# A graph layer over a dense adjacency on one core: one shift of the quick weights on GpSimd, two pairs of copies ordered, the order of all work drawn anew

## The chip, the cores and the metric

The kernel runs on one core of one Trainium2 chip. The time is device microseconds of one execution; three runs of the kernel before took 192.53, 192.82 and 192.81 us, median 192.81. The profile is of a fourth execution, of 192.34 us, whose span from the first to the last instruction is 190.6 us.

## What is computed

The reference, cut to what matters (4096 nodes, 64 features, an adjacency `adj` of 4096 x 4096 float32 zeros and ones):

```python
h = maximum(layernorm(x), 0)
support = h @ weight
mask = (adj != 0)
rank = cumsum(mask, axis=1)
deg = rank[:, -1:]
k = minimum(deg, 100)
pos = rank - (deg - k)
w = mask * where(pos > 0, 0.5 ** (k - pos), 0)
out = x + (w @ support + bias)
```

`k - pos` is the number of neighbours that stand further right in the same row. So each neighbour is weighted by a power of two whose exponent is a count of ones behind it, and only the last 100 neighbours of a row count.

## The kernel before

**Tiles and units.** The adjacency is 64 MB and is read once, as 64 tiles of 128 rows by 2048 columns (1 MB each). Four tiles that cover 512 rows and one half of the columns are a unit; there are 16 units, `u` = 0 to 15, two for each of eight groups `g` of 512 rows. A group's right half comes first, because counts run from the right. Unit 15 is the left half of the last group; its tiles are 60 to 63.

**The way of a tile n.** `load` (L120, SP's queue, eight buffers) brings it. `convert` packs four columns as bytes into one 32-bit word (L341 on DVE; for the tiles in `signed` L339 on ACT, with one more bit operation in `settle`, L361). `transpose` turns 128x128 words through TensorE into PSUM (L352). `settle` copies them to `mt` (L363, DVE).

**The way of a unit u.** `totals` sums the bytes over short stretches (L369, PE). Two bytes of these sums are turned to float16: the first by `split` (L379, ACT), the second by `divide` (L382, DVE), both out of the same PSUM tile and into the two halves of one tile `sums`. In a left half `carry` (L388, GpSimd) puts the counts of the right half into row 0. `suffix` (L396, PE) adds what lies behind each stretch, and `clamp` (L400, DVE) limits that to 100. `place` (L407 and L412, PE) adds the counts within a stretch and leaves in each of four PSUM tiles `v` two bytes per element that are the exponents; a unit has two calls of it, for k = 0 to 3 and for k = 4 to 7. There are five buffers `v`, taken in turn.

**Weights and sums.** For each k `weigh` (L420, ACT) makes the weights by one exponential of 128x1024 values. `aggregate` (L457, PE) multiplies them with the features `hr` into the accumulator of the group, two matmuls for each k. In the last unit k = 5, 6, 7 are weighed and multiplied in two halves of 256 rows each (third argument 0 and 1). Three weights, `QUICK` = (14,4), (15,0), (15,4), are made on DVE instead: `encode` (L426) multiplies the count by minus 2^23 and limits it, `cut` (L431) adds 100 times 2^23 so that the integer is the bit pattern of the power of two, `take` (L435) copies that to the type of the matmul; `gather` is their `aggregate`, with features that `lower` (L443, GpSimd) has scaled.

**The end of a group.** `drain` adds the bias and copies the accumulator to SBUF (L473 on ACT), `turn_back` transposes it (L480), `finish` adds it to x (L487 and L488, DVE). For the last group, g = 7, all three come in two halves: the drain's first half on ACT, its second on DVE (L471), and each half has its own store (L490). `store` (L495) writes the other rows from SP's queue, behind the loads.

**What sets the order.** A planner at the end of the function lists every step as `task(step, arguments, engine, rank, hold, lag, needs, pool)`. `hold` and `lag` are the nanoseconds for which a step is taken to hold its engine and until its result is there; `needs` are the steps before it. `shift` and `own` are tables that move the rank of a kind of step and of a single step. A loop builds the order: it takes the engine that can start soonest and, among the steps that it could start within that engine's window (`wait`), the one of lowest rank.

```python
free = [1200, 3400, 4000, 5500, 800]
wait = 250, 60, 250, 60, 0
...
_, at, kind = min((rank, at, kind) for at, rank, e, kind in heads if e == engine and at <= soon + wait[engine])
```

The times of the planner live only in it. What reaches the chip is the order of instructions on each engine, which is kept, and semaphore waits for the data and the buffers.

Of the kernel before, what the change touches and what calls it, by code (L numbers as in the profile page):

```python
# [13 lines left out]
I32 = mybir.dt.int32  # L14
# [3 lines left out]
ALU = mybir.AluOpType  # L18
# [13 lines left out]
def kernel(  # L32
# [34 lines left out]
    nc = tc.nc  # L67
# [260 lines left out]
    low, codes, masks, words, wts, accs, tots, pts, sums8, behind, vs, signed = {}, {}, {}, {}, {}, {}, {}, {}, {}, {}, {}, (2, 8)  # L328
# [100 lines left out]
    def cut(u, k):  # L429

        nc.vector.tensor_scalar(codes[u, k][:, 1].bitcast(I32), codes[u, k][:, 0].bitcast(I32), 100 * 2.0 ** 23, None, op0=ALU.add)  # L431
# [60 lines left out]
    def store(r):  # L492
# [8 lines left out]
    shift = {"aggregate": 45, "carry": -26.5, "center": 25, "clamp": -23.5, "constants": 43.5, "convert": 36, "cut": 18.5,  # L501
             "divide": 0.5, "drain": -44.5, "encode": -1, "finish": -29.5, "first": -47.5, "halved": 5, "lower": 10.5,
             "order_of": 19.5, "power": -19.5, "relu": 39.5, "root": 26.5, "scale": 31, "second": 23.5, "settle": -26,
             "split": -38.5, "spread": 12, "square": 48.5, "store": 8, "suffix": 25, "support": 70, "take": -12, "totals": -32,
             "transpose": -15.5, "turn": 20, "turn_back": 62, "turned": 29, "weigh": 24}
    own = {
           "aggregate": {(0, 0): 6, (0, 3): -2, (0, 4): -16, (0, 6): -11, (1, 0): 7, (1, 1): -18, (1, 5): -5, (1, 7): -9, (11, 4): 10, (11, 5): 14, (11, 6): 6, (11, 7): -1, (12, 0): -20, (12, 3): 4, (12, 4): -2, (12, 5): -4, (12, 6): -10, (13, 1): -10, (13, 2): 6, (13, 3): 8, (13, 4): 1, (13, 5): -12, (13, 6): -4, (13, 7): -12, (14, 0): 2, (14, 1): 1, (14, 2): -16, (14, 3): -11, (14, 4): 15, (14, 5): -8, (14, 6): 18, (14, 7): -36, (15, 2): -4, (15, 3): -2, (15, 4): 1, (15, 5): 1, (15, 5, 0): -1, (15, 5, 1): -6, (15, 6): 8, (15, 6, 0): 7, (15, 6, 1): -3, (15, 7): -2, (2, 1): 4},
           "carry": {(1,): -2, (13,): 6, (15,): 3, (3,): 29}, "center": {(0,): 1, (1,): 2, (2,): 1, (3,): 3},
           "clamp": {(0,): -13, (1,): -8, (13,): 7, (15,): -14, (2,): -8, (3,): -2}, "constants": {(0,): -17, (1,): 15},
           "convert": {(1,): 20, (12,): -12, (13,): 4, (14,): -4, (16,): 19, (17,): 8, (18,): -16, (19,): -4, (2,): -9, (20,): -1, (4,): 5, (5,): 9, (57,): -16, (58,): -5, (59,): 8, (6,): -1, (60,): -5, (61,): -1, (7,): 1, (8,): 16, (9,): 8},  # L510
           "count": {(2,): 1}, "counted": {(2,): -18, (4,): 8}, "cut": {(14, 4): 15},
           "divide": {(0,): 24, (1,): 2, (14,): 8, (15,): -14, (2,): 15, (3,): -4},
           "drain": {(0,): 8, (5,): -22, (6,): 6, (7, 0): 7, (7, 1): 4}, "encode": {(14, 4): -9},
           "finish": {(5,): 7, (6,): -33, (7, 0): 4, (7, 1): -1}, "first": {(0, 0): -1, (1, 0): 1, (1, 1): 8},
           "halved": {(0,): -3, (1,): -5, (13,): 4, (14,): -9, (2,): 4}, "lower": {(15, 0): -3}, "order_of": {(2,): 4, (4,): 3},
           "place": {(0, 0): -8, (0, 1): -8, (1, 0): -13, (12, 1): 1, (13, 0): 8, (13, 1): -2, (14, 0): -9, (14, 1): 5, (15, 0): -26, (15, 1): 2, (2, 0): -4, (2, 1): 16},
           "power": {(): -23}, "relu": {(0,): -4, (1,): -3, (2,): 8}, "root": {(): -7}, "scale": {(3,): -6},
           "second": {(0, 0): -6, (0, 1): -1, (1, 1): 22},
           "settle": {(1,): -4, (10,): 2, (11,): 1, (12,): -9, (13,): 19, (15,): 2, (17,): -2, (18,): -19, (19,): -6, (2,): -11, (3,): 6, (4,): -11, (5,): -4, (56,): 5, (57,): 22, (58,): -2, (59,): 5, (6,): 1, (61,): -4, (63,): -4, (9,): 1},
           "split": {(0,): 5, (1,): -9, (13,): 3, (14,): 9, (15,): 3, (2,): -1, (3,): -12},  # L520
           "spread": {(0,): 10, (1,): 14, (2,): -9, (3,): -1}, "square": {(1,): 10, (2,): -5, (3,): -12},
           "store": {(0,): -13, (1,): -3}, "suffix": {(1,): 3, (13,): -36, (14,): -6, (15,): -1}, "support": {(0,): -3, (2,): 15},
           "take": {(15, 0): -4, (15, 4): -2},
           "totals": {(0,): -1, (1,): -4, (13,): 3, (14,): -4, (15,): 10, (2,): -2, (3,): 7, (4,): -15},
           "transpose": {(0, 0, 2): 4, (0, 2, 4): -9, (1, 0, 2): -8, (10, 0, 2): -16, (11, 0, 2): 7, (11, 2, 4): 14, (12, 0, 2): -2, (12, 2, 4): -18, (13, 0, 2): -1, (13, 2, 4): 4, (14, 0, 2): -16, (15, 0, 2): -1, (15, 2, 4): 5, (16, 2, 4): -14, (17, 0, 2): -12, (18, 0, 2): 29, (18, 2, 4): 29, (19, 0, 2): 16, (19, 2, 4): -4, (2, 0, 2): -2, (2, 2, 4): 1, (3, 2, 4): -15, (4, 0, 2): 3, (4, 2, 4): 21, (5, 0, 2): -4, (5, 2, 4): -4, (56, 0, 2): 1, (56, 2, 4): -1, (57, 0, 2): -27, (58, 0, 2): 1, (58, 2, 4): 8, (59, 0, 2): 5, (6, 0, 2): 25, (6, 2, 4): 37, (60, 2, 4): -7, (61, 0, 2): 10, (61, 2, 4): 6, (63, 0, 2): -8, (7, 0, 2): -2, (8, 0, 2): -1, (8, 2, 4): -16, (9, 2, 4): -1},
           "turn": {(0, 0): -12, (0, 12): 10, (0, 4): 2, (0, 8): 3, (1, 0): -25, (1, 4): -16},
           "turn_back": {(5,): 4, (6,): -22, (7, 0): 8}, "turned": {(0, 0): 2, (0, 12): 6, (1, 12): -6, (1, 4): 12, (1, 8): 14},
           "weigh": {(0, 2): 8, (0, 3): 3, (0, 4): 3, (0, 5): 4, (0, 7): -16, (1, 0): 22, (1, 3): -3, (1, 4): 1, (1, 7): 2, (12, 3): 8, (12, 4): -8, (12, 5): -6, (12, 6): -22, (12, 7): 6, (13, 0): 2, (13, 1): -12, (13, 2): 23, (13, 5): 10, (13, 6): -8, (13, 7): 5, (14, 3): -3, (14, 5): -4, (14, 7): -8, (15, 2): -4, (15, 3): -11, (15, 5, 0): 3, (15, 5, 1): -19, (15, 6): 7, (15, 6, 0): -3, (15, 6, 1): -4, (15, 7): -5, (15, 7, 0): 4, (15, 7, 1): 3, (2, 0): 2, (2, 1): 4, (2, 3): -7, (2, 4): 8, (2, 6): 2, (2, 7): -1, (3, 0): -4, (3, 1): 1}}
# [50 lines left out]
    for u, (g, c0, cb) in enumerate(UNITS):  # L579
# [3 lines left out]
        task(divide, (u,), DVE, at - 2.5, 600, 720, [("totals", u)])  # L583
# [5 lines left out]
        for k in range(2 * cb):  # L589
            due = at + k  # L590
            if k % 4 == 0:
                task(place, (u, k // 4), PE, due, 800, 920, [("clamp", u), ("constants", 1)], ("v", *(("encode" if (u, k + j) in QUICK else "weigh", u, k + j, *((1,) if u == U - 1 and k + j in PARTED else ())) for j in range(4))))
            if u == U - 1 and k in PARTED:
                continue
            weighs = "weigh"
            piece_of = block(u, k) // (HB // 2)
            if (u, k) in QUICK:
                weighs = "take"
                task(encode, (u, k), DVE, due - 8, 1150, 1270, [("place", u, k // 4), ("convert", NT - 2)])
                task(cut, (u, k), DVE, due - 8, 650, 770, [("encode", u, k)])  # L600
                task(take, (u, k), DVE, due - 8, 650, 770, [("cut", u, k)], ("w", ("gather", u, k)))
                task(lower, (u, k), POOL, due - 8, 1200, 1300, [("second", piece_of // 2, piece_of % 2), ("convert", NT - 3)])
            else:
                task(weigh, (u, k), ACT, due + 2.5, 1000, 1130, [("place", u, k // 4)], ("w", ("aggregate", u, k)))
            task(gather if (u, k) in QUICK else aggregate, (u, k), PE, due + 14, 480, 720, [(weighs, u, k), ("lower", u, k) if (u, k) in QUICK else None, ("second", piece_of // 2, piece_of % 2)] +
                 ([("drain", g - 1)] if g and head and k == 0 else []))
        for part in range(2 if u == U - 1 else 0):
            for k in PARTED:
                due = at + k + part
                task(weigh, (u, k, part), ACT, due + 2.5, 520, 650, [("place", u, k // 4)], None if part else ("w", ("aggregate", u, k, 1)))  # L610
                task(aggregate, (u, k, part), PE, due + 14, 260, 500, [("weigh", u, k, part)])
        if c0 == 0:
# [5 lines left out]
            else:  # L618
                for part in range(2):
                    task(drain, (g, part), DVE if part else ACT, at, 300, 350, [("aggregate", u, PARTED[-1], part), *(("gather", *uk) for uk in QUICK)])  # L620
# [9 lines left out]
    wait = 250, 60, 250, 60, 0  # L630
    landed, taken, order = 0, {p: [] for p in places}, []
    while kinds:
# [16 lines left out]
        if f in (load, fetch):  # L649
            lag = max(landed - at, 2450) + (1280 if f is fetch else 620 * UNITS[UT[args[0]][0]][2])  # L650
            lag += 1400 if key == ("load", 6) else 0
# [49 lines left out]
```

## Time and profile before

| | us | |
|---|---|---|
| median of three runs | 192.81 | 192.53 to 192.82 |
| span of the profiled execution | 190.6 | granted TensorE clock 0.98 |
| PE busy | 172.4 | 90% of the span, 1504 matmuls |
| DVE busy | 165.6 | 87%, 225 instructions |
| ACT busy | 158.1 | 83%, 175 instructions |
| GpSimd busy | 19.7 | 10%, 60 instructions |
| `weigh`, L420, 128x1024 | 126.7 | 122 x 1120 ns |
| `convert` on DVE, L341 | 86.2 | 62 x 1393 ns |
| `convert` on ACT, L339 | 5.0 | 2 x 2511 ns |
| `settle`, L363 | 42.2 | 62 x 681 ns |
| `split`, L379 / `divide`, L382 | 9.6 / 11.0 | 16 x 598 / 16 x 685 ns |
| `encode` / `cut` / `take` | 3.7 / 2.1 / 2.1 | 3 x 1224 / 693 / 691 ns |

Read it as an average over a stretch with transfers and a tail without them. Busy shares of 83 to 90% on three engines say that no engine is idle for long, not which of them sets the end. The slices of the span, the landing times of the loads and the waits in the last 23 us tell that. A matmul's recorded end is modelled, and recorded spans of GpSimd are rough. An ACT instruction's recorded span overlaps the next one's by about 0.1 us, so a row of them is counted by the spacing of starts.

### The profile page before, as it was taken

What the parts mean: (1) busy time and instruction counts of PE and PEld (TensorE: products, weight loads), DVE (VectorE), ACT (ScalarE), POOL (GpSimd) and SP (SyncE); (2) the same over time, 40 slices, a digit from 0 to 9 for tenths busy, and PEclk for the clock granted to TensorE, in tenths of its full rate; (3) what the DMA queues carried; (4) which work ended last, traced back from release to release, by engine and by line L of the source; (5) the groups of instructions that cost most, each with busy time, mean ns of one, the idle gap of its engine ahead of it and who ended that gap; (6) DMA issues with size and microseconds to landing.
All of it is one profiled execution on the core that took longest, in us unless ns stands there. A gap on an engine that the chain in (4) does not pass through costs nothing.

```text
span 190.6 us, 3811 instructions
## 1 busy us (share of the span) xinstructions
PE 172.4 (90%) x1504; PEld 106.5 (56%) x1504; DVE 165.6 (87%) x225; ACT 158.1 (83%) x175; POOL 19.7 (10%) x60
## 2 busy tenths in 40 slices
PE   7799999787988999999999989999999898989981
PEld 5676959254644565556664645655565454644460
DVE  4853886999999998999999988999999999988753
ACT  2289219999897899889987999989989799998880
POOL 7000062100000000100010002000100058001000
PEclk9999859999999999999999999999999999999999
DMA  6999999999999999999999999999999999902000
GB/s 211 418 419 423 418 419 428 409 418 423 423 413 423 425 413 425 423 414 425 421 411 426 421 414 425 423 419 416 423 416 418 423 418 418 381 27 83 0 3 28
DMA packets 10338, 69.49 MB, mean 365 GB/s; under 512 B 1360, under 2 KB 1616, under 8 KB 2128
## 3 DMA queue, kind: packets, MB, share of 16 engines
q1 hardware_dynamic: 10016, 69.15, 87.8%
q8 instruction: 12, 0.20, 0.4%
q10 hardware_dynamic: 304, 0.10, 0.2%
q14 instruction: 6, 0.05, 0.1%
HBM read 68.19 MB, written 1.05 MB: 363 GB/s over the span
## 4 chain that ended last, share of the span: by engine, by line
PE 45%; ACT 14%; DVE 13%; issue 12%; DMA 8%; POOL 7%; POOLq 0%; ACTq 0%; DVEq 0%
PE acc L457 16%; ACT wk L420 11%; PE pt L352 9%; DMA a_sb<-in_adj_dram 8%; DVE m L341 5%; PE v L412 4%; PE v L407 4%; POOL low L443 3%; PE tot L369 2%; PE ps L396 2%; PE pd L281 2%; DVE mt L363 2%; PE pc L265 2%; PE px L256 2%; DVE xs L307 1%
## 5 line engine op out<-in xcount | busy, mean ns | idle before, releaser
L420 ACT ACTIVATE wk<-v,floor 128x1024 fp32r<-128x1024 uint8 (+1 forms) x128 | 130.2, 1101 | 13.1 <-PE v L412 12.8
L341 DVE TENSOR_SCALAR m<-a_sb 128x2048 uint8<-128x2048 f32 x62 | 86.2, 1393 | 2.6 <-DMA a_sb<-in_adj_dram 2.6
L457 PE MATMUL acc<-wk,hr 128*128 128x512 f32 (+1 forms) x256 | 78.5, 421 | 1.4 <-ACT acc_sb L473 0.9
L457 PEld LDWEIGHTS acc<-wk,hr 128*128 128x128 f32 x256 | 43.2, 189 | 14.6 <-issue 3.3
L352 PE MATMUL pt<-ident,m 128*128 128x128 f32 x256 | 42.2, 286 | 6.9 <-DVE m L341 2.8
L363 DVE COPY mt<-pt 128x512 uint32<-128x512 uint32 x62 | 42.2, 681 | 5.8 <-PE pt L352 5.7
L352 PEld LDWEIGHTS pt<-ident,m 128*128 128x128 f32 x256 | 28.5, 143 | 25.2 <-issue 8.2
L388 POOL COPY sums<-behind 1x512 f16<-1x512 f16 x8 | 6.1, 766 | 133.5 <-ACT sums L379 133.5
L407 PE MATMUL v<-behind,where 32*128 32x512 f16 x128 | 14.8, 390 | 1.2 <-DVE behind L400 0.6
L412 PE MATMUL v<-mt,tri 32*32 32x512 f16 x512 | 14.4, 401 | 0.0
L379 ACT ACTIVATE sums<-tot 128x512 f16<-128x512 uint8 x16 | 9.6, 598 | 5.1 <-DVE sums L382 2.7
L400 DVE TENSOR_SCALAR behind<-ps,excess 128x512 f16<-128x512 f32 x16 | 11.9, 743 | 0.8 <-PE ps L396 0.7
L382 DVE CAST sums<-tot 128x512 f16<-128x512 uint8 x16 | 11.0, 685 | 1.6 <-ACT sums L379 0.9
L396 PE MATMUL ps<-sums,later 128*128 128x512 f16 x32 | 10.1, 398 | 0.8 <-POOL sums L388 0.7
L369 PE MATMUL tot<-mt,band 128*32 128x512 f16 x128 | 10.2, 393 | 0.1
L412 PEld LDWEIGHTS <-tri 32*32 32x32 f16 x512 | 4.4, 88 | 10.0 <-issue 10.0
L407 PEld LDWEIGHTS <-where 32*128 32x128 f16 x128 | 3.7, 91 | 10.6 <-issue 10.6
L248 PE MATMUL none<-junk 128*128 128x256 bf16 x49 | 8.0, 334 | 1.1 <-DVE junk L133 1.1
L260 ACT ACTIVATE mt<-px 64x512 f32<-64x512 f32 x8 | 4.2, 585 | 4.8 <-PE px L256 4.8
L248 PEld LDWEIGHTS <-junk 128*128 128x128 bf16 x49 | 5.8, 120 | 3.2 <-DVE junk L133 1.1
L473 ACT ACTIVATE acc_sb<-acc,bias_sb 128x512 f32<-128x512 f32 (+1 forms) x8 | 5.3, 664 | 1.5 <-PE acc L457 1.4
L480 PE MATMUL po<-ident,acc_sb 128*128 128x128 f32 x30 | 4.8, 280 | 1.4 <-ACT acc_sb L473 1.4
(88 smaller groups left out, 98.6 us busy)
## 6 DMA issues: line engine op xcount, KB each, us to landing
a_sb<-in_adj_dram SPq DMA_DIRECT2D x64, 1024.0 KB, 15.6
xr<-in_x_dram SPq DMA_DIRECT2D x2, 512.0 KB, 6.3
out_dram<-xr SPq DMA_DIRECT2D x1, 512.0 KB, 18.6
out_dram<-xr SPq DMA_DIRECT2D x1, 384.0 KB, 2.3
out_dram<-xr ACTq DMA_DIRECT2D x1, 64.0 KB, 1.6
out_dram<-xr SPq DMA_DIRECT2D x1, 64.0 KB, 1.6
w<-in_L_gnn_weight_dram ACTq DMA_DIRECT2D x2, 16.0 KB, 6.0
bias_sb<-in_L_gnn_bias_dram SPq DMA_DIRECT2D x1, 0.2 KB, 15.7
```

What stands on the lines that cost most here:

```text
L248: nc.tensor.matmul(none[:, :2 * P], junk[:, :P], junk, start=True, stop=True)
L341: nc.vector.tensor_scalar(m_v, a_v, 0.0, 64.0, op0=ALU.not_equal, op1=ALU.add)
L352: nc.tensor.transpose(pts[n][:, c, :], m32[:, c * P:(c + 1) * P], ident)
L363: nc.vector.tensor_copy(mw, pt)
L369: nc.tensor.matmul(tot[SUB * c:SUB * (c + 1), :], band[:, SUB - 12 - 4 * a:2 * SUB - 12 - 4 * a], masks[u][:, c, :, a], start=(a == 0), st ...
L382: nc.vector.tensor_copy(*bytes_of(u, 1))
L396: nc.tensor.matmul(px, later[cb][:r, f, :], sums[:r, f, :], start=(f == 0), stop=(f == 1))
L400: nc.vector.tensor_scalar(behind[u], pts.pop((u, "s")), excess[UNITS[u][2]], float(MAX_NEIGH), op0=ALU.subtract, op1=ALU.min)
L407: nc.tensor.matmul(v, where[q, a, :], behind[u][q, :], start=True, stop=False, skip_group_check=True)
L412: nc.tensor.matmul(vs[u, 4 * a + j][SUB * c:SUB * (c + 1), :], tri[q, q], m, start=False, stop=True, skip_group_check=True)
L420: nc.scalar.activation(wts[u, k][:, :, r], v.bitcast(U8).rearrange("p (i f) -> p f i", f=4)[:, :2, r], AF.Exp, scale=-LN2, bias=floor)
L457: nc.tensor.matmul(accs[g][:, r], parts.rearrange("p s d -> p (s d)"), wk[:, s, r], start=(k == s == 0 and c0 + cb * E * P == N), stop=(c0 ...
```

## The change

It has these parts.

- `signed` has the tiles 0, 1, 6 and 13 instead of 2 and 8: four converts run on ACT, sixty on DVE.
- `cut` is issued on GpSimd instead of DVE, for all three quick weights.
- `divide` needs `split` in the planner, instead of `totals`; `drain` of the last group's second half needs the first half.
- The holds and lags of `divide`, `encode`, `take`, the halved `weigh` and the halved `drain` are larger, ACT's window in the planner is 150 instead of 250, and the landing of load 54 is taken to be 1400 later, as that of load 6 already was.
- Nearly all entries of `shift` and `own` are other numbers.

```diff
-    low, codes, ..., signed = {}, {}, ..., (2, 8)
+    low, codes, ..., signed = {}, {}, ..., (0, 1, 6, 13)
...
-        nc.vector.tensor_scalar(codes[u, k][:, 1].bitcast(I32), codes[u, k][:, 0].bitcast(I32), 100 * 2.0 ** 23, None, op0=ALU.add)
+        nc.gpsimd.tensor_scalar(codes[u, k][:, 1].bitcast(I32), codes[u, k][:, 0].bitcast(I32), 100 * 2.0 ** 23, None, op0=ALU.add)
...
-    shift = {"aggregate": 45, "carry": -26.5, "center": 25, "clamp": -23.5, ...
+    shift = {"aggregate": 60, "carry": -21, "center": 30, "clamp": -28, ...
...
-        task(divide, (u,), DVE, at - 2.5, 600, 720, [("totals", u)])
+        task(divide, (u,), DVE, at - 2.5, 610, 730, [("split", u)])
...
-                task(encode, (u, k), DVE, due - 8, 1150, 1270, [...])
-                task(cut, (u, k), DVE, due - 8, 650, 770, [("encode", u, k)])
-                task(take, (u, k), DVE, due - 8, 650, 770, [("cut", u, k)], ("w", ("gather", u, k)))
+                task(encode, (u, k), DVE, due - 8, 1160, 1300, [...])
+                task(cut, (u, k), POOL, due - 8, 1800, 1900, [("encode", u, k)])
+                task(take, (u, k), DVE, due - 8, 690, 820, [("cut", u, k)], ("w", ("gather", u, k)))
...
-                task(weigh, (u, k, part), ACT, due + 2.5, 520, 650, ...)
+                task(weigh, (u, k, part), ACT, due + 2.5, 570, 700, ...)
...
-                    task(drain, (g, part), DVE if part else ACT, at, 300, 350, [..., *(("gather", *uk) for uk in QUICK)])
+                    task(drain, (g, part), DVE if part else ACT, at, 420, 500, [..., *(("gather", *uk) for uk in QUICK), ("drain", g, 0) if part else None])
...
-    wait = 250, 60, 250, 60, 0
+    wait = 250, 60, 150, 60, 0
...
-            lag += 1400 if key == ("load", 6) else 0
+            lag += 1400 if key in (("load", 6), ("load", 54)) else 0
```

The order that comes out for the end of the program, step by step on each engine:

```
DVE before: convert 61, settle 60, divide 14, clamp 14, convert 62, settle 61, convert 63, settle 62, settle 63, finish 6,
            divide 15, encode (14,4), cut (14,4), clamp 15, take (14,4), encode cut take (15,0), encode cut take (15,4), drain (7,1)
DVE after:  convert 61, settle 60, divide 14, convert 62, clamp 14, settle 61, convert 63, settle 62, settle 63, finish 6,
            divide 15, encode (14,4), clamp 15, encode (15,0), take (14,4), encode (15,4), take (15,0), take (15,4), drain (7,1)
ACT before: drain 6, weigh (14,2), (14,3), split 15, weigh (14,5), (14,6), (14,7), (15,1), (15,2), (15,3), six halves, drain (7,0)
ACT after:  drain 6, weigh (14,2), split 15, weigh (14,3), (14,5), (14,6), (14,7), (15,1), (15,2), (15,3), six halves, drain (7,0)
PE before:  aggregate (13,6), (13,7), transposes 63, turn_back 6, aggregate (14,0), totals 15, place (14,1), aggregate (14,1), (14,2),
            suffix 15, aggregate (14,3), (14,5), (14,6), place (15,0), gather (14,4), aggregate (14,7), (15,1), place (15,1), ...,
            aggregate (15,5,1), gather (15,4), aggregate (15,6,1), (15,7,1)
PE after:   aggregate (13,6), transposes 63, aggregate (13,7), totals 15, turn_back 6, aggregate (14,0), place (14,1), aggregate (14,1), (14,2),
            suffix 15, aggregate (14,3), (14,5), place (15,0), aggregate (14,6), (14,7), (15,1), place (15,1), gather (14,4), ...,
            aggregate (15,5,1), (15,6,1), (15,7,1), gather (15,4)
GpSimd after: carry 13, lower (three times), carry 15, cut (14,4), cut (15,0), cut (15,4)
```

SP issues the same 64 loads in the same order, with the small load of the bias one tile earlier.

## The prediction

> **What bounds the kernel now.** I first read the page's slices, because they say whether anything but the transfers sets the pace.
>
> ```profile
> DMA  6999999999999999999999999999999999902000
> GB/s 211 418 419 423 418 419 428 409 418 423 423 413 423 425 413 425 423 414 425 421 411 426 421 414 425 423 419 416 423 416 418 423 418 418 381 27 83 0 3 28
> ```
>
> From the second slice (4.8 us) to the 34th the DMA engines are full and move about 419 GB/s, and then they stop. The landing records of the trace put tiles 61, 62 and 63, the last of the adjacency, at 162.88, 165.36 and 167.83 us: 2.48 us a tile, without a hole. No order of the engines makes that stream faster; it could only starve it. What a new order can shorten is the 22.8 us from 167.83 to the end at 190.6. So I read that stretch on the two engines that the chain of waits names there, ACT and DVE. Columns: start, length, engine, line, operation, tiles, idle time ahead and its releaser.
>
> ```profile
> 170.36 0.69 ACT L473 ACTIVATE acc_sb<-acc,bias_sb 128x512 f32<-128x512 f32 x1
> 170.93 2.13 ACT L420 ACTIVATE wk<-v,floor 128x1024 fp32r<-128x1024 uint8 x2
> 173.63 0.60 ACT L379 ACTIVATE sums<-tot 128x512 f16<-128x512 uint8 x1 [0.57 <-DVE sums L382]
> 174.13 3.12 ACT L420 ACTIVATE wk<-v,floor 128x1024 fp32r<-128x1024 uint8 x3
> 177.91 6.68 ACT L420 ACTIVATE wk<-v,floor 128x1024 fp32r<-128x1024 uint8 x9 [0.67 <-PE v L412]
> 185.18 0.47 ACT L473 ACTIVATE acc_sb<-acc,bias_sb 128x256 f32<-128x256 f32 x1 [0.59 <-PE acc L457]
> ```
>
> ACT has no hole from 164.29 to the end of its weights at 184.59 but 0.57 us (split(15) waits for divide(15)) and 0.67 us (weigh(15,1) waits for place(15,0)). Those 1.24 us are all that ACT can give back in the tail.
>
> ```profile
> 172.91 0.69 DVE L382 CAST sums<-tot 128x512 f16<-128x512 uint8 x1 [0.23 <-PE tot L369]
> 173.58 1.22 DVE L426 TENSOR_SCALAR code<-v 128x1024 int32<-128x1024 uint8 x1
> 174.84 0.69 DVE L431 TENSOR_SCALAR code<-code 128x1024 int32<-128x1024 int32 x1
> 175.57 0.75 DVE L400 TENSOR_SCALAR behind<-ps,excess 128x512 f16<-128x512 f32 x1
> ...
> 180.91 1.23 DVE L426 TENSOR_SCALAR code<-v 128x1024 int32<-128x1024 uint8 x1 [0.35 <-PE v L412]
> 182.17 0.69 DVE L431 TENSOR_SCALAR code<-code 128x1024 int32<-128x1024 int32 x1
> 182.97 0.69 DVE L435 CAST wk<-code 128x1024 fp32r<-128x1024 f32 x1
> ```
>
> The last quick weight (encode, cut, take) takes 2.75 us, 180.91 to 183.66, and its matmuls end before those of ACT's last half (184.64 to 185.14): about 1.0 us of slack.
>
> The waits show two pairs that never run together; columns: total us, times, longest.
>
> ```profile
> ACT sums L379 <- DVE sums L382: 2.7, 6, 0.6
> DVE acc_part L471 <- ACT acc_sb L473: 2.0, 1, 2.0
> ```
>
> Last, GpSimd: one line's durations (min/median/max in ns), and a copy of 512 values alone (174 us) and beside DVE (155 us).
>
> ```profile
> L443 POOL TENSOR_SCALAR low<-hr x6: 518/520/1627, 156.0 to 160.7; 128x128 fp32r<-128x128 f32 x6
> 154.85 1.18 POOL L388 COPY sums<-behind 1x512 f16<-1x512 f16 x1 [20.29 <-ACT sums L379]
> 174.29 0.60 POOL L388 COPY sums<-behind 1x512 f16<-1x512 f16 x1 [13.07 <-ACT sums L379]
> ```
>
> **What the Trainium skill says.** "GPSIMD Engine Reference", section on performance versus the Vector engine, gives about 1.8 cycles an element at 1.2 GHz as the best case for elementwise loops; no row here has 1024 elements, the three above lie on both sides of it. "SBUF", section "Who interferes with whom", says that GpSimd and a DVE copy, cast or tensor_scalar in a two-port mode exclude each other for a whole instruction. The trace agrees: the copy goes from 0.60 to 1.18 us, the multiply from 0.52 to 1.63 us, and one convert beside it from 1.39 to 1.75 us.
>
> **The change part by part.** The durations are those of the one profiled execution (span 190.6 us, that run 192.34 us; the other three 192.53 to 192.82). I work out a difference on that span and add it to the median.
>
> 1. *Four converts on ACT instead of two.* DVE loses 2 x 1.39 = 2.78 us, ACT gains 2 x 2.51 = 5.02 us. Three of the four now stand ahead of weigh(0,0), before one: ACT idles 4.6 us before 8.35 and 5.9 us before 27.89. Tile 0 lands at 5.6, tile 6 at 24.5; both converts fit there. Between 28 and 60 us ACT has one either way (8 before, 13 after). From 40 to 170 ACT idles some 10 us in sum, mostly waiting for v, so a lag of the start is absorbed. Cost at the end: nothing, hidden by the transfers.
>
> 2. *Divide after split.* The pair is serial already (the waits above), so only which is first changes. For unit 15 split no longer waits 0.57 us for DVE. Its other 15 uses lie beside the transfers: nothing.
>
> 3. *The new order from 167.83 us on.* Convert(63) starts at 168.07 as before. Clamp(14) now stands behind convert(62), which can't start before 165.36: 165.4 + 1.3 + 0.7 = 167.5, so place(14,0) ends near 168.4 (was 168.2), in time for weigh(14,0) at 168.4. Transposes of 63 end at 170.24 as before; aggregate(13,7) is now behind them, to 170.7, so drain(6) starts at 170.75 (was 170.36). Totals(15) comes ahead of turn_back(6), at 171.05 (was 172.15). ACT from there, by the spacing of starts (drain 0.57, weigh 1.0, split 0.5): weigh(14,2) 171.3, split(15) 172.3, then (14,3), (14,5), (14,6), (14,7) at 172.85, 173.85, 174.85, 175.85. DVE: finish(6) after turn_back(6), 172.4 to 173.25; divide(15) to 174.0; encode(14,4) to 175.2; clamp(15), whose suffix waits on PE behind two aggregates to 175.3, 175.35 to 176.1. Place(15,0) follows at 176.2; its fifth-last v buffer, freed by weigh(14,6) at 176.0, doesn't hold it. Weigh(15,1) at 177.1 instead of 177.91: **0.8 us earlier**, and ACT's last weight ends at 183.8, its matmuls at 184.35.
>
> 4. *Cut on GpSimd.* DVE loses 3 x 0.69 = 2.07 us; the chain of each quick weight gets the difference of a GpSimd and a DVE operation. No trace here prices a 1024-element GpSimd operation. Below: 0.60 us for 512 gives 1.2. Above: the slope between the 32-element row (0.29 us) and the 128-element one (0.52) is 2.4 ns an element, which gives 2.7 us. The skill's 1.8 cycles give 1.54 us, plus about 0.25 us fixed: I take **1.8 us, an estimate**. Below nothing is excluded: the operation replaced took 0.69. Cut(14,4) ends at 177.1 and cut(15,0) near 180.8 (it waits out take(14,4)); both are needed later. Cut(15,4) is not hidden. Place(15,1) needs the v buffer of weigh(15,2), as before, and ends at 180.1; encode(15,4) 180.15 to 181.4; then take(15,0), 0.69, and cut(15,4) want the shared port: one after the other, 181.4 + 0.69 + 1.8 = 183.9 whichever is first; take(15,4) to 184.6 and its two matmuls, now last on PE, to 185.3.
>
> 5. *Drain's halves in turn.* The second already starts at 185.69, 0.04 after the first ends: nothing. GpSimd has nothing queued behind cut(15,4); behind take(15,4) on DVE is the drain's second half, which needs the same matmuls anyway. The changed holds, lags, the window of ACT and the mark on load 54 act through the order alone. SP keeps its loads in order and both stores behind them; one small bias load moves ahead by one tile.
>
> Sum: ACT gains 0.8 and the quick weight ends 185.3 against 185.14: **+0.2 us**, the drain at 185.4 instead of 185.18. Span 190.8, time 193.0.
>
> **The rivals.** *B: the last cut is hidden.* If it takes 1.2 us, or take(15,0) doesn't shut it out, take(15,4) is done by 184.0 and its matmuls follow ACT's last ones directly, to 184.8: -0.35 us; where the drain of group 6 also comes 0.25 us earlier, -0.6. That gives 192.2 to 192.5, I say 192.4. For it: the copy's 0.60 us. Against it: the contended rows.
> *C, slower: GpSimd becomes the end of the path.* One mechanism, at cut(15,4): 2.7 us as the multiply's slope has it, ends 184.8; take 185.5, matmuls 186.2: +1.1 us, 193.9. It decides from the point where cut takes over 1.6 us behind take(15,0), since then the gather ends after 185.1. For it: the 0.52 us for 128 elements. Against it: the copy.
> *D: the new order arrives late.* PE is 98% busy from 160 to 170 us; if totals(14) or place(14,0) comes 0.6 us late there, the whole weight stream moves: 0.2 + 0.6, 193.6. Against it: the same work, and the transfers pace it.
> That the change does nothing of what it says is a rival only for the pairs of 2 and 5, which I cost at nothing already.
>
> **How the numbers follow.** My case A 0.37, B 0.34, C 0.17, D 0.12. This kernel's measurement tells about 0.2% (0.39 us) from no change. A is within it but for 0.07; of B 0.26 lies below it. Faster 0.26; same 0.30 + 0.08 = 0.38; slower 0.07 + 0.17 + 0.12 = 0.36. The range takes B down to 192.2 and C up to 194.1, and leaves out a tenth at each end. A alone spans 192.8 to 193.3.
>
> **What would show it.** Right: the last load lands near 167.8; split(15) ahead of divide(15) without ACT's wait; weigh(15,1) near 177.1; L431 on GpSimd near 1.8 us; the last matmuls before the drain are those of gather(15,4), and PE waits for its take there. Wrong: a landing of the last tile later than 168.5 (the transfers starved), L431 under 1.2 or over 2.7 us, ACT's last weight ending after 184.6 (D), or a hole of ACT in the tail that isn't named here.

## The result and the profile after

The changed kernel takes **193.6 us** (median of four runs, 193.33 to 193.69), the kernel before in the same measurement 192.81 us (192.53 to 193.09): 1.0039 times as long, 95% interval 1.0021 to 1.0056. It is slower by 0.8 us. The time lies in the stated range, 192.2 to 194.1, but not in the likeliest case of it, which said 193.0 and a difference too small to measure. It lies beside the slower rivals, C at 193.9 and D at 193.6, and the time alone can't tell the two apart; the lines below and the experiments do.

The profiled execution has a span of 191.6 us (193.33 us as a run). Its slices of the transfers first:

```profile
DMA  6999999999999999999999999999999999702000
GB/s 221 415 426 421 414 422 424 419 414 421 422 417 424 419 419 419 421 417 422 424 416 417 422 417 422 422 419 422 416 414 421 422 416 424 308 12 82 0 3 27
```

They are full as before, and the last tile lands at 167.91 us (167.83 before). From the landing to the end it is 23.7 us instead of 22.8. The last quick weights, on DVE (columns: start, length, engine, line, operation, tiles, idle time ahead and its releaser):

```profile
180.45 1.23 DVE L426 TENSOR_SCALAR code<-v 128x1024 int32<-128x1024 uint8 x1 [1.27 <-PE v L412]
181.84 1.52 DVE L435 CAST wk<-code 128x1024 fp32r<-128x1024 f32 x1 [0.17 <-POOL code L431]
184.59 0.69 DVE L435 CAST wk<-code 128x1024 fp32r<-128x1024 f32 x1 [1.23 <-POOL code L431]
```

And the durations of L431, now on GpSimd (min/median/max in ns):

```profile
L431 POOL TENSOR_SCALAR code<-code x3: 2776/2782/3153, 175.4 to 181.8; 128x1024 int32<-128x1024 int32 x3
178.66 5.90 POOL L431 TENSOR_SCALAR code<-code 128x1024 int32<-128x1024 int32 x2 [0.48 <-DVE code L426]
```

The second line is cut(15,0) and cut(15,4) in one row; the last one runs from 181.77 to 184.55. Where `cut` took 0.69 us it now takes 2.78. `encode(15,4)` ends at 181.68, 0.46 us earlier than before, but `take(15,4)` starts at 184.59 instead of 182.97. PE and ACT show what waits for it:

```profile
183.41 0.74 PE L457 MATMUL acc<-wk,low 128*128 128x512 f32 x2 [0.98 <-DVE wk L435]
183.99 1.11 PE L457 MATMUL acc<-wk,hr 128*128 128x256 f32 x8
185.34 0.73 PE L457 MATMUL acc<-wk,low 128*128 128x512 f32 x2 [0.24 <-DVE wk L435]
```

```profile
173.31 10.82 ACT L420 ACTIVATE wk<-v,floor 128x1024 fp32r<-128x1024 uint8 x13
186.17 0.47 ACT L473 ACTIVATE acc_sb<-acc,bias_sb 128x256 f32<-128x256 f32 x1 [2.04 <-PE acc L457]
```

The two matmuls at 185.34 are `gather(15,4)`, the last work before the drain. ACT's weights run without a hole (one row of 13 where before there were two rows with 0.67 us between them) and end at 184.13, before at 184.59. Then ACT idles 2.04 us where it had idled 0.59. So the order gained at ACT, and behind it the cut lost more. The drain starts at 186.17, 0.99 us later than before.

### The profile page after: what moved, and what is told of

The parts are those of the page before. It is cut to its first block, busy times and chain, and to the rows that moved or that the text cites. A ratio compares the mean times of both kernels' runs of the same rounds, so it can differ in the third digit from the quotient of the medians.

```text
span 191.6 us, 3801 instructions
## 1 busy us (share of the span) xinstructions
PE 173.8 (91%) x1499; PEld 107.3 (56%) x1499; DVE 161.2 (84%) x220; ACT 162.5 (85%) x177; POOL 28.7 (15%) x63
## 4 chain that ended last, share of the span: by engine, by line
PE 53%; DVE 19%; ACT 14%; issue 6%; POOL 4%; POOLq 2%; ACTq 0%
PE acc L457 17%; PE pt L352 12%; ACT wk L420 9%; DVE m L341 9%; PE v L412 5%; PE v L407 4%; DVE mt L363 4%; POOL code L431 3%; PE tot L369 3%; PE ps L396 3%; PE pp L304 2%; PE pd L281 2%; PE pc L265 2%; PE po L480 2%; POOLq L697 1%
## 5 line engine op out<-in xcount | busy, mean ns | idle before, releaser
L341 DVE TENSOR_SCALAR m<-a_sb 128x2048 uint8<-128x2048 f32 x60 | 82.9, 1388 | 2.9 <-DMA a_sb<-in_adj_dram 2.9
L363 DVE COPY mt<-pt 128x512 uint32<-128x512 uint32 x60 | 40.6, 680 | 5.1 <-PE pt L352 5.0
L352 PE MATMUL pt<-ident,m 128*128 128x128 f32 x256 | 40.7, 284 | 4.3 <-DVE m L341 3.4
L352 PEld LDWEIGHTS pt<-ident,m 128*128 128x128 f32 x256 | 29.8, 144 | 19.7 <-PE acc L457 4.8
L407 PE MATMUL v<-behind,where 32*128 32x512 f16 x128 | 15.6, 390 | 1.2 <-ACT wk L420 0.9
L339 ACT ACTIVATE m<-a_sb 128x2048 int8<-128x2048 f32 x4 | 10.1, 2534 | 1.8 <-DMA a_sb<-in_adj_dram 1.8
L431 POOL TENSOR_SCALAR code<-code 128x1024 int32<-128x1024 int32 x3 | 8.7, 2904 | 1.8 <-DVE code L426 1.8
L248 PE MATMUL none<-junk 128*128 128x256 bf16 x44 | 6.9, 328 | 1.1 <-DVE junk L133 1.1
L361 DVE TENSOR_SCALAR mt<-pt 128x512 uint32<-128x512 uint32 x4 | 2.8, 690 | 5.3 <-PE pt L352 5.3
```

The source lines that it names most:

```text
L341: nc.vector.tensor_scalar(m_v, a_v, 0.0, 64.0, op0=ALU.not_equal, op1=ALU.add)
L352: nc.tensor.transpose(pts[n][:, c, :], m32[:, c * P:(c + 1) * P], ident)
L363: nc.vector.tensor_copy(mw, pt)
L407: nc.tensor.matmul(v, where[q, a, :], behind[u][q, :], start=True, stop=False, skip_group_check=True)
L431: nc.gpsimd.tensor_scalar(codes[u, k][:, 1].bitcast(I32), codes[u, k][:, 0].bitcast(I32), 100 * 2.0 ** 23, None, op0=ALU.add)
```

## The experiments

Each is the named kernel with the edit shown and nothing else. Where a step is moved, `ahead(a, b)` gives step `a` of the finished order the place just ahead of step `b`. The kernel before was measured again beside each group, on three chips: medians of 192.88, 192.99 and 192.85 us, with single executions from 191.85 to 194.16.

### Cut back on DVE, in the changed kernel

```diff
-        nc.gpsimd.tensor_scalar(codes[u, k][:, 1].bitcast(I32), ...)
+        nc.vector.tensor_scalar(codes[u, k][:, 1].bitcast(I32), ...)
```

> The changed kernel with cut back on DVE at the same places of the order; nothing else. Theory (the GpSimd cut of 2.8 to 3.2 us, at the last quick weight, is what the change loses, and the new order alone gains): take(15,4) ends near 183.7 instead of 185.3, the last matmuls are still gather(15,4), behind ACT's last half (184.7), so the drain starts near 185.2 instead of 186.17: about 1.0 us less than the changed kernel, 192.6 us, that is 0.2 us under the kernel before. Rival (the new order itself arrives late, cut's engine hardly matters): 193.4 to 193.7, as the changed kernel.

Measured: 192.95 us, 1.0001 times the kernel before (0.9984 to 1.0019). The loss is gone with the engine of one instruction. From the start of convert(63) to the start of the drain this profile has 16.76 us, the changed kernel's 17.66: 0.90 less, near the 1.0 expected. The medians, of two measurements, differ by 0.65. The 0.2 us under the kernel before that the theory expected did not come: here convert(63) starts at 168.73, later than in the profiles of the kernel before (168.07) and of the changed kernel (168.50), and the part on the prediction comes back to that. The gather is still last:

```profile
183.14 1.78 PE L457 MATMUL acc<-wk,hr 128*128 128x256 f32 x8
184.76 0.63 PE L457 MATMUL acc<-wk,low 128*128 128x512 f32 x2
```

Now nothing waits ahead of it: the eight half matmuls run up to it, and it costs only its own 0.6 us, because it stands behind them.

### The same, and the gather where the kernel before has it

```diff
+    ahead(('gather', 15, 4), ('aggregate', 15, 6, 1))
+    ahead(('take', 15, 4), ('gather', 15, 4))
```

> As the run with cut on DVE, and gather(15,4) ahead of aggregate(15,6,1) on PE, where the kernel before has it. Theory: the end is then ACT's last weight (184.1) and its own two half matmuls, to 184.7; drain at 184.75, 1.4 us less than the changed kernel: 192.15 us, 0.6 under the kernel before. Rival (the end is set by something ahead of ACT's last weight, or gather's place is worth nothing): the same as with cut on DVE alone, within 0.15 us.

Measured: 192.62 us, 0.999 (0.997 to 1.001). The drain starts 0.90 us after ACT's last weight, in the run before 1.13, and it is 16.53 us from the start of convert(63) to the drain instead of 16.76. So in the profiles the place of the gather is worth 0.23 us; the medians differ by 0.33 us where 0.45 were expected. By its interval this version isn't told apart from the kernel before, and the 0.6 us under it that the theory expected did not come.

```profile
183.66 0.73 PE L457 MATMUL acc<-wk,low 128*128 128x512 f32 x2 [0.20 <-DVE wk L435]
184.22 0.63 PE L457 MATMUL acc<-wk,hr 128*128 128x256 f32 x4
```

### Only the last cut on DVE

```diff
-        nc.gpsimd.tensor_scalar(codes[u, k][:, 1]...)
+        (nc.vector if (u, k) == QUICK[-1] else nc.gpsimd).tensor_scalar(codes[u, k][:, 1]...)
```

> The changed kernel with the last cut, that of (15,4), back on DVE and the other two left on GpSimd. Theory (only the last one is on the path; the others are needed later than they end): the same as all three on DVE within 0.2 us, 192.6. Rival (GpSimd's cuts cost through the port that they share with DVE's copies, or gather(15,0) is late too and holds PE): between 192.9 and 193.6.

Measured: 192.75 us, 0.9993 (0.9973 to 1.0012). Two GpSimd cuts of 2.8 and 3.2 us remain and cost nothing that can be measured, so it is the one of (15,4) that the change pays for. take(15,0) waits 0.17 us for the second one, which costs nothing at the end:

```profile
182.24 0.69 DVE L435 CAST wk<-code 128x1024 fp32r<-128x1024 f32 x1 [0.17 <-POOL code L431]
182.84 0.69 DVE L431 TENSOR_SCALAR code<-code 128x1024 int32<-128x1024 int32 x1
183.63 0.69 DVE L435 CAST wk<-code 128x1024 fp32r<-128x1024 f32 x1
```

### Cut on GpSimd in the kernel before

The reverse of the first edit, in the kernel before.

> The kernel before with cut on GpSimd, at the same places of its order; nothing else. There each take stands right behind its cut and ahead of the next encode, so the three chains follow each other. With cut at 2.8 us: take(14,4) from 177.7, take(15,0) from 182.5, take(15,4) from 187.3, its matmuls and the two behind them to 189.2 instead of 185.14: 4.1 us more, 196.9. With the 1.8 us that the prediction took: take(15,4) from 184.7, 1.4 us more, 194.2.

Measured: 196.89 us, 1.0212 (1.0171 to 1.0252). The price of 2.8 us carries through three chains that follow each other, take for take. In DVE's timeline the two idle times are those of the cuts:

```profile
182.87 0.69 DVE L435 CAST wk<-code 128x1024 fp32r<-128x1024 f32 x1 [2.89 <-POOL code L431]
183.48 1.22 DVE L426 TENSOR_SCALAR code<-v 128x1024 int32<-128x1024 uint8 x1
187.59 0.69 DVE L435 CAST wk<-code 128x1024 fp32r<-128x1024 f32 x1 [2.89 <-POOL code L431]
```

So the new order hides two of three such cuts; in the order of before, the change of engine alone costs 4 us.

### The price of the cut: halved, and as an integer addition

```diff
-        nc.gpsimd.tensor_scalar(codes[u, k][:, 1]..., codes[u, k][:, 0]..., 100 * 2.0 ** 23, ...)
+        for e, b in ((nc.gpsimd, 0), (nc.vector, 1)):
+            e.tensor_scalar(codes[u, k][:, 1, b]..., codes[u, k][:, 0, b]..., 100 * 2.0 ** 23, ...)
```

> The changed kernel with each cut in two: the first 512 values on GpSimd, the other 512 on DVE. If the GpSimd time is per element (2.4 to 2.6 ns and some 0.2 us fixed): 1.4 to 1.6 us for 512, and take(15,4) starts near 183.6 instead of 184.6: 192.6 to 192.9 us, as with cut on DVE. If it is mostly a fixed cost of this operation: over 2 us for 512, take(15,4) after 184.0, 193.2 or more.

Measured: 192.68 us, 0.9988 (0.9975 to 1.0001).

```profile
L432 POOL TENSOR_SCALAR code<-code x3: 1598/1864/1868, 175.9 to 182.3; 128x512 int32<-128x512 int32 x3
L432 DVE TENSOR_SCALAR code<-code x3: 416/832/834, 176.6 to 182.7; 128x512 int32<-128x512 int32 x3
```

At the shortest, 512 values take 1.60 us (beside `clamp` and DVE's own half) and 1024 take 2.78 (2.77 to 2.78 with DVE idle too, in the kernel before with cut on GpSimd). From these two, (2.78 - 1.60) / 512 = 2.3 ns an element and 0.4 us fixed, an estimate. So most of the price is per element, near the slope of the small rows, 2.4 ns. The longer durations in these rows are of halves that ran beside each other or beside `take`. take(15,4) started at 184.16, not near 183.6, but convert(63) started 0.52 us later than in the profile of the changed kernel; with that taken off it is 183.64.

```diff
+    hundred = setup.tile([P, 1], I32, name="hundred")
+    nc.gpsimd.memset(hundred, 100 << 23)
...
-        nc.gpsimd.tensor_scalar(codes[u, k][:, 1]..., codes[u, k][:, 0]..., 100 * 2.0 ** 23, None, op0=ALU.add)
+        nc.gpsimd.tensor_tensor(codes[u, k][:, 1]..., codes[u, k][:, 0]..., hundred.to_broadcast([P, 2 * W]), op=ALU.add)
```

> The changed kernel with cut on GpSimd as an integer addition of two tensors (the codes and one value repeated) instead of a tensor and a scalar. If the 2.8 us come from carrying the integers through float and back, the integer form is shorter: 1.5 to 2.3 us, and the kernel 192.7 to 193.2. If they are the price of 1024 elements with reading, adding and writing, the second input adds to it: 2.8 us or more, and the kernel 193.6 or more.

Measured: 193.12 us, 1.0021 (1.0 to 1.0043).

```profile
L433 POOL TENSOR_TENSOR code<-code,hundred x3: 1892/2269/2269, 175.7 to 182.1; 128x1024 int32<-128x1024 int32 x3
```

The integer form, with one more input, takes 1.89 us at the shortest, two thirds of the form with a scalar. That fits the first of the two expectations; what happens inside was not looked at. The time follows the price again: 0.5 us shorter at cut(15,4) (2.27 against 2.78), 0.52 from convert(63) to the drain (17.14 against 17.66), about 0.5 us shorter as a whole than the changed kernel.

### The order of the tail alone, in the kernel before

```diff
+    ahead(('split', 15), ('divide', 15))
```

> The kernel before with split(15) ahead of divide(15), nothing else. Theory (the hole of 0.57 us on ACT closes, but divide, encode, cut and clamp(15) behind it on DVE come 0.7 us later, so place(15,0) starts at 177.05 instead of 176.96): the same as before within 0.2 us. Rival (the order of the two halves by itself is the gain): 0.5 us less.

Measured: 192.94 us, 0.9997 (0.9982 to 1.0013). Split first closes one hole, divide and clamp(15) then wait on DVE, and the hole opens again ahead of weigh(15,1), with 0.99 us:

```profile
174.28 0.62 ACT L379 ACTIVATE sums<-tot 128x512 f16<-128x512 uint8 x1
175.03 3.13 ACT L420 ACTIVATE wk<-v,floor 128x1024 fp32r<-128x1024 uint8 x3
179.15 1.12 ACT L420 ACTIVATE wk<-v,floor 128x1024 fp32r<-128x1024 uint8 x1 [0.99 <-PE v L412]
```

```diff
+    ahead(('totals', 15), ('aggregate', 14, 0))
+    ahead(('turn_back', 6), ('aggregate', 14, 0))
+    ahead(('split', 15), ('weigh', 14, 3))
+    ahead(('clamp', 15), ('cut', 14, 4))
```

> The kernel before with four steps of its order moved, nothing else: totals(15) and turn_back(6) change places and stand ahead of aggregate(14,0), split(15) stands ahead of weigh(14,3) and of divide(15), clamp(15) ahead of cut(14,4). Cut stays on DVE. Theory (the tail's order is what the change has right, and it can be had without its cut and without its other ranks): split(15) at 172.0, weigh(15,1) at 177.0 to 177.3 instead of 177.91, ACT's last weight at 183.7 to 184.0, the drain at 184.3 to 184.6: 0.6 to 0.9 us less than the kernel before. Rival (ACT's gain comes from the new ranks as a whole, or place(15,0) waits for something else): within 0.3 us of the kernel before.

Measured: 192.53 us, 0.9982 (0.9968 to 0.9995), the one version here that is told apart from the kernel before as faster, by 0.2%. It gains from four moved steps and none of the new ranks. The size is under the 0.6 to 0.9 us expected (0.46 us between the medians, 0.53 from convert(63) to the drain, 16.58 against 17.11): weigh(15,1) still waits 0.67 us for place(15,0), which in this order stands behind aggregate(14,6).

```profile
173.20 4.31 ACT L420 ACTIVATE wk<-v,floor 128x1024 fp32r<-128x1024 uint8 x4
178.17 6.68 ACT L420 ACTIVATE wk<-v,floor 128x1024 fp32r<-128x1024 uint8 x9 [0.67 <-PE v L412]
```

### Two converts back on DVE

```diff
-        if n in signed:
+        if n in (0, 6):
```

in both places of `convert` and `settle`; the order is that of the changed kernel.

> The changed kernel with converts 1 and 13 on DVE again at the same places of the order, so two converts on ACT as before. Theory (these lie beside the transfers and the lag of the start is absorbed): the same as the changed kernel, 193.6, within 0.2 us. Rival (DVE, 2.8 us more loaded, comes late to the last tiles): convert(63) later by up to 2.8 us, 194 to 196; or (ACT, 5 us less loaded, was late): less than 193.2.

Measured: 194.38 us, 1.0062 (1.0039 to 1.0084), single executions from 192.95 to 195.52. The theory fell: on DVE these converts are not free. Three more runs sought the cause, with one convert back at a time (`n in (0, 6, 13)` for convert 1, `n in (0, 1, 6)` for convert 13) and with a second profile of this kernel.

> The changed kernel with convert 1 alone back on DVE, at its place in the order (the run with converts 1 and 13 back was 0.6% over the kernel before and spread over 2.5 us). Theory (it lies in the first 15 us, where DVE and ACT both have holes): as the changed kernel, 193.6, within 0.2 us, with its narrow spread. Rival (the start is what made that run slow): 194.0 or more and a spread over 1.5 us.

Measured: 193.71 us, 1.0038 (1.0022 to 1.0054), 193.18 to 194.02: as the changed kernel, as the theory had it.

> The changed kernel with convert 13 alone back on DVE, at its place in the order. Theory (it stands near 46 us, where DVE has no hole and still works off the backlog of the start; 1.4 us more there delays the converts that free the buffers of the loads): 194.0 or more and a spread over 1.5 us, as with both back. Rival (convert 1 is the cause, or only both together): 193.6 within 0.2 us.

Measured: 193.88 us, 1.0054 (1.0025 to 1.0084), 192.93 to 195.54: the spread of the executions is back, 2.6 us against 0.8 with convert 1 alone, so the spread comes with convert 13. The medians of the two can't be told apart, and the 194.0 expected was not reached. Nor is it by the transfers, as the theory had it: the second profile shows that.

> One more look at the kernel with converts 1 and 13 back on DVE, for a profile of one of its longer executions, since the profile had was of a short one (193.08 of a median of 194.38). If it falls at 194 or more: theory (the transfers starve) says that the last load lands more than 0.5 us after 167.9; rival (DVE or ACT reach the last tiles late) says that it lands at 167.9 and convert(63) starts over 1.2 us later.

This execution took 194.6 us. The last tile lands at 168.23, and DVE comes to it 1.46 us later, without a hole ahead:

```profile
168.44 0.73 DVE L400 TENSOR_SCALAR behind<-ps,excess 128x512 f16<-128x512 f32 x1
169.09 0.68 DVE L363 COPY mt<-pt 128x512 uint32<-128x512 uint32 x1
169.69 1.38 DVE L341 TENSOR_SCALAR m<-a_sb 128x2048 uint8<-128x2048 f32 x1
```

The rival was right in the main. convert(63) starts 1.45 us later than in the shorter execution (169.69 against 168.24); 0.3 of that is the landing (168.23 against 167.92), the rest is DVE. From convert(63) to the drain both have the same, 17.67 and 17.68 us. From the landing records and the starts of the converts, the lag of convert n behind its tile, in us:

| kernel, half TensorE clock at the start | n = 13 | 20 | 40 | 50 | 60 | 63 |
|---|---|---|---|---|---|---|
| before, 6.8 us | 5.4 | 3.8 | 3.1 | 3.0 | 1.4 | 0.2 |
| before with split(15) first, 6.8 and 3.4 us | 5.8 | 5.0 | 4.1 | 4.2 | 2.8 | 1.6 |
| changed, 10.2 us | 5.0 | 3.2 | 1.7 | 0.9 | 1.1 | 0.6 |
| changed, converts 1 and 13 on DVE, none | 3.9 | 2.9 | 1.2 | 0.5 | 0.9 | 0.3 |
| the same, second profile, 10.2 us | 5.2 | 4.2 | 2.7 | 1.9 | 2.0 | 1.5 |
| changed, convert 13 on DVE, none | 3.8 | 2.9 | 1.3 | 0.3 | 1.7 | 1.1 |
| changed, convert 1 on DVE, 3.4 us | 3.9 | 2.0 | 0.4 | 0.1 | 1.4 | 0.8 |

In the two rows with 10.2 us of half clock the lag is nearly equal up to tile 13 (5.0 and 5.2). The convert there, 1.4 us of DVE or none, parts them by 1.0 us, and 0.9 of that is still there at tile 63.

The last two rows show the limit of this. There DVE had nearly caught up at tile 50 and then idled for a landing, 1.2 to 1.3 us ahead of convert(53): in every profile one tile there, 53 or 54, lands 3.6 to 4.2 us after the one before it, while 2.5 us is usual. At tile 63 both are later than the changed kernel all the same. So the lag of the start is not all that counts there, and why the executions with convert 13 on DVE spread so far is shown for one pair of profiles only.

## Why the prediction was right, and where it was wrong

**The frame held, and the range.** That the time lies in the range is owed to the slower rivals, which the range took in; the likeliest case missed by 0.6 us. The last tile lands between 167.7 and 168.2 us in all fourteen profiles; nothing starved the transfers. What differs lies in the tail and in how late DVE comes to tile 63. From the start of convert(63) to the start of the drain the profiles have 17.11 us before, 17.66 changed, 16.76 with cut on DVE and 16.53 with the gather ahead too. The difference of 0.99 us between the two profiled drains is then this sum: convert(63) 0.43 us later (168.50 against 168.07); the new order 16.76 - 17.11 = -0.35; the GpSimd cut 17.66 - 16.76 = +0.90. The last two are firm: five profiles with this tail and the cut on GpSimd have 17.66 to 17.68, three with cut(15,4) off that path 16.73 to 16.76. The first is of two single executions, and the start of convert(63) varies by 1.45 us with one and the same kernel (168.24 and 169.69 above). By the medians, 0.79 us in all and 0.55 of it in the tail, some 0.24 us are left for it, an estimate.

**Step 4 failed in a size.** The prediction took 1.8 us for the cut, worked out from the skill's best case, and kept the row's slope, 2.7 us, as the upper bound. The bound was the measurement: 2.78 us. With it the working of step 4 gives take(15,4) at 184.9; measured 184.59. The mechanism was as written, the end of the path at cut(15,4) and gather(15,4) last on PE, and so was the point from which it decides, 0.69 + 1.6 us after encode(15,4): the halved cut ended 1.95 us after it and the kernel was not slower than before, the whole one 2.87 us (181.68 to 184.55). The rival C had the size of the cut.

That the step missed take(15,4) by no more is luck. It let cut(15,4) wait for take(15,0), 0.69 us, which did not happen (below), and that made up for most of the 0.98 us by which the cut was priced too low: from the end of encode(15,4) to the end of the cut it had 2.49 us, measured 2.87. The figure of the Trainium skill ("GPSIMD Engine Reference", performance versus the Vector engine) lost to the slope of two rows of this very kernel, one of them a GpSimd operation with a scalar as the cut is; that was the choice to make otherwise.

**One assumption of step 4 was wrong.** It had take(15,0) and cut(15,4) one after the other. They ran beside each other: cut from 181.77 to 184.55, its 2.78 us as when alone, and take from 181.84 to 183.36, 1.52 instead of 0.69. Take was held up for 0.83 us, not for the whole of cut; so it is in all five profiles that have this pair (1.51 to 1.52 us). The Trainium skill's page "SBUF — State Buffer", section "Who interferes with whom", has the loser wait for the full instruction; here it didn't, by these records, of which those of GpSimd are rough.

**Step 3 held in its mechanism, with over half the gain.** Split ran without a wait, ACT had no hole after it, weigh(15,1) started at 177.44. Predicted was 177.1, before was 177.91: 0.47 us gained instead of 0.8. The missing part is convert(63), which the step let start at 168.07 as before: counted from it, weigh(15,1) came after 8.94 us where the step had 9.03 and the kernel before has 9.84. It is not the reordered copies behind convert(61). In the kernel before divide(14) stands ahead of convert(61), not where the list of orders has it, but in both kernels the same eight steps (converts 60 to 62, settles 59 to 61, divide and clamp of unit 14) fill DVE without a hole up to convert(63): 6.87 us from 161.20 before, 6.89 us from 161.61 after. DVE was late ahead of them. The last long hole is at divide(13), here before and after:

```profile
155.46 0.68 DVE L382 CAST sums<-tot 128x512 f16<-128x512 uint8 x1
155.54 0.69 DVE L382 CAST sums<-tot 128x512 f16<-128x512 uint8 x1 [0.82 <-ACT sums L379]
```

In the new order split(13) stands on ACT behind drain(5) and two weighs. It starts at 154.89, 1.6 us after totals(13) has ended (153.27), and DVE idles 0.82 us for it, up to 155.54. With an earlier split the divide would have filled that hole and been out of the way when tile 58 landed at 155.50. From there to convert(63) DVE has no hole at which it could catch up. The chain of waits, followed back from the end of the program, comes through this divide and this split (between 168.0 and 173.5 us it has a stretch that it doesn't explain). The ten profiles of the changed order all have this wait, 0.62 to 0.88 us; the four of the order before have none, and one hole of 0.24 us behind that place. That is rival D in small, at another place than it named: on DVE, not on PE. No run took this wait out, so what it costs at the end is argued, not shown; in the profile of the changed kernel it could be 0.6 us at most, since that is all by which convert(63) lags its tile.

**Step 1 was right on what was changed and wrong in its reason.** It said that a lag of the start is absorbed, so that the two converts cost and give nothing. With convert 13 back on DVE it was not absorbed in the execution with 10.2 us of half clock at the start. Taking that convert off DVE was worth something: the changed order reaches tile 50 with a lag of 0.9 us where the kernel before still has 3.0. About 1.0 us of that is the convert, since with converts 1 and 13 back, as many on DVE as before, the lag is 1.9. At tile 63 nothing of the lead is left (0.6 and 0.2). That two more converts on ACT cost nothing at the end fits these runs.

**Step 2 held where it was tried, and step 5 held.** Split ahead of divide in unit 15 by itself gives 0.9997. That the other uses cost nothing is doubtful: the wait at divide(13) is one of them, though there split was first in the kernel before too (154.20, divide at 155.46). The drain's second half started 0.04 us after the first ended, before and after.

**The forecast of no change** had 0.38, slower 0.36, and slower it was. The sum was +0.2 with the cut at 1.8; with the measured 2.78 and the rest as it stood it would have been +1.2. The profiles show +0.99, the medians +0.8: the cut did not wait for take(15,0), and the gain of the order was eaten up in part by the late convert(63).

What stays open: why a GpSimd addition with a scalar takes longer than one with a second tensor; what the wait at divide(13) costs, and whether the planner's new need for split or the new ranks put split(13) so late; and what the new ranks are worth as a whole.

## What to carry to other kernels

Work that is moved to an idle engine is priced at that engine's rate, and it is free only where a later step needs its result later than that: of three equal cuts two were free and the third cost 0.9 us. Where the profile has two rows of an engine with the same kind of operation and different sizes, their slope is a better price than a general figure. And a busy engine that is "hidden by the transfers" may carry a delay to the last tile: in one pair of profiles 0.9 us of a convert at 47 us was still there at 168, with DVE 97% busy from 45 to 143 us. So may a wait of 0.8 us at 155 us that has no hole behind it. Look at the lag behind the landings and at the last hole, not at the busy share.

## What the runs showed of the hardware

- A GpSimd tensor_scalar addition on int32 took 2.78 us for 128x1024 and 1.60 for 128x512, a GpSimd tensor_tensor addition on int32 1.89 us for 128x1024, each at its shortest; on DVE the tensor_scalar took 0.69 and 0.42.
- A DVE copy issued 0.07 us after a GpSimd operation of 2.78 us took 1.52 us instead of 0.69 and ended 1.19 us before it. A GpSimd cut issued 0.17 us after such a copy took 3.15 us.
- TensorE's clock was halved for 3.4 to 10.2 us between 20 and 50 us in twelve of the fourteen profiles, differently from execution to execution. In the two kernels with convert 13 on DVE the longest times go with the lowest clock: 192.9 to 194.4 us where the mean clock of the execution was 0.987 or more, 194.7 to 195.5 where it was 0.969 or less. With convert 1 alone there it is 193.2 to 194.0 at any clock, from 0.966 to 0.997.
